# A graph network's message passing: four moves in the kernel's first iterations

## The chip, the core and the metric

The kernel runs on one core of a Trainium2 chip. The time is that of one execution on the device, in microseconds (us). The core's engines work side by side, each through its own list of instructions in order: TensorE (PE in the profile; its weight loads are PEld), VectorE (DVE), ScalarE (ACT), GpSimd (POOL), and SyncE (SP), which here only issues transfers. An engine waits where an instruction needs a result that another engine or a transfer has not delivered yet, or a buffer that another engine has not read yet.

## The reference

128 graphs of 64 nodes with 128 features each. For every pair of nodes (i, j) a message is computed by a small network of three layers with a ReLU and a layer normalisation after each of the first two; messages are kept where the adjacency matrix has a one, and summed over j. A second network of the same form takes the node and its sum, and its result is added to the node.

```python
def _mlp(x, w0, b0, g0, be0, w1, b1, g1, be1, w2, b2):
    h = jax.nn.relu(x @ w0 + b0)
    h = _layernorm(h, g0, be0)
    h = jax.nn.relu(h @ w1 + b1)
    h = _layernorm(h, g1, be1)
    return h @ w2 + b2
...
        f_i = jnp.broadcast_to(part_feats[:, :, None, :], (B, P, P, C))
        f_j = jnp.broadcast_to(part_feats[:, None, :, :], (B, P, P, C))
        pair_feats = jnp.concatenate([f_i, f_j], axis=-1)
        messages = _mlp(pair_feats, msg_w0, msg_b0, msg_ln0_g, msg_ln0_b, msg_w1, msg_b1, msg_ln1_g, msg_ln1_b, msg_w2, msg_b2)
        messages = messages * coupling_matrix[..., None]
        agg = jnp.sum(messages, axis=2)
        upd_in = jnp.concatenate([part_feats, agg], axis=-1)
        updated = part_feats + _mlp(upd_in, upd_w0, upd_b0, upd_ln0_g, upd_ln0_b, upd_w1, upd_b1, upd_ln1_g, upd_ln1_b, upd_w2, upd_b2)
```

About one pair in eight has an edge, so the kernel computes messages for the edges alone.

## The kernel before

**Units of work.** Each graph gets 640 places for edges: five tiles of 128. Two graphs are a pair (index p, 64 of them), two pairs a quad (index q, 32), four pairs a block (index b, 16). The edges are worked through in chunks of four tiles: five chunks to a quad, 160 in all. An iteration n of the main loop (line 1039) works on several chunks at once, each in another stage.

**The stages of a chunk.** `layer0(n)` (line 529) multiplies the chunk's one-hot selection matrix S by the block's rows, in two parts each (a high and a low part, `abh` and `abl`), into the PSUM bank `hps`; the ReLU on ACT (L538) empties it. `stats0` (line 540) transposes the result on PE into the bank `hT` (L544), from which DVE takes the statistics of every edge (L548). Eight iterations after layer0 comes `layer1` (line 595): a product with the bias table and the roots (L602), or four seeds by ACT (L593) instead, then four tile products (L605), and a ReLU (L608). `stats1`, `weights` and `reduce` end the messages; the class `Unit` computes the update of a block.

**What a quad needs ahead of layer1.** `var0_of(q)` (line 554) makes the variances of its 20 tiles from the statistics of its five chunks, by `square_sum` (five small POOL instructions, L245 to L249). `root_of(q)` takes the root on ACT (L255), splits it into a high part (ACT, L562) and a low part (POOL, L563); `turn_root` transposes it on PE (L568), `root_out` copies it (L573). The bias table `b1t`, made once, comes from `bias_table` (line 638: one ACT cast, L643, and four POOL instructions, L645 to L649) and five calls of `bias_part` (line 653, one POOL instruction each, L655).

**What makes S.** For a pair, `distance` (ACT, L478) and `make_tp` (DVE, L484) make the selection of its nodes; `node_rows` casts it (on ACT for the first pairs, L491, on POOL later), and `stack` sends it into S by two transfers. `marks` (PE, L509) and `compare` (DVE, L517) make the other half.

**Rows.** `rows(b, half)` (line 443) multiplies a block's nodes by the two halves of the first layer's weights into one PSUM bank (L449, L451); `rows_hi` (ACT, L463) and `rows_lo` (DVE, L469) read it. The banks at issue are `mu` (handed out by `ubank`), which `rows` uses and in which the derived weights of the early iterations are made, and `ma` (`abank`), used by `count`, `turn_x`, `turn_root` and others. Each has one buffer, so a new user waits until the last one's readers are done.

**Derived weights.** `derivation` (line 170) lists 13 small matrices made on the chip, such as `w2c` and `u2c` (L180) and `bu1b` (L203, L204). Each has an ACT step one iteration ahead, a PE product, and a copy out of PSUM one iteration later.

**The order of the work** is written by hand. `at(n, place, fn, ...)` enters a call in iteration n at a named place; within a place calls run in the order in which they were entered. The loop runs the places in this order, and each engine's instructions follow it:

```python
for n in range(last + 1):
    run(n, "a")
    run(n, "m")
...
        layer1(n - L1)
    run(n, "b")
...
        layer0(n if n >= QC else n + LEAD)
...
    run(n, "k")
...
    for k in ("x", "x1", "x2", "e0", "e1", "e"):
        run(n, k)
```

Before the loop a prologue runs chunks 0 to 2. Iterations 0 and 1 run layer0 of chunks 3 and 4; iterations 2 to 4 have no layer0; iteration 5 runs chunk 5, and from there iteration n runs chunk n. Quad 0's statistics end with chunk 4's, in iteration 3; layer1 of chunk 0 is in iteration 8. Block 0's second half of rows, `rows(0, 1)`, is in iteration 3 and is first needed by chunk 5.

**Unread products.** `keep_busy(k)` (line 909) issues k products of a constant matrix with itself into the bank `ys`, which nothing reads before the first `reduce` in iteration 18. In float32 each product is two matmuls. The prologue has 25 of them (50 matmuls at L912).

Of the kernel before, what the change touches and what calls it, by code (L numbers as in the profile page):

```python
# [23 lines left out]
def tile_gnn(  # L24
# [52 lines left out]
    PB = 4  # L77
# [207 lines left out]
    def edge_path(es):  # L285
# [18 lines left out]
        def abank():  # L304

            return ps_a.tile([P, 512], F32, name="ma")

        def ubank():

            return ps_u.tile([P, 512], F32, name="mu")  # L310
# [13 lines left out]
        def at(n, place, fn, *args):  # L324
            plan.setdefault((n, place), []).append((fn, args))
# [117 lines left out]
        def rows(b, half, k0=0, k1=4):  # L443

            blk = blocks[b]
            ps = blk["ab_ps", half] if k0 else ubank()
            for k in range(k0, k1):
                s = slice((4 * half + k) * N, (4 * half + k + 1) * N)
                nc.tensor.matmul(ps[0:N, k * C:(k + 1) * C], lhsT=blk["xnT"][:, s], rhs=w0a,  # L449
                                 start=True, stop=True)  # L450
                nc.tensor.matmul(ps[N:P, k * C:(k + 1) * C], lhsT=blk["xnT"][:, s], rhs=w0b,  # L451
                                 start=True, stop=True)
            blk["ab_ps", half] = ps
# [354 lines left out]
        for b in range(NB):  # L808
            o = b * CPB
            if b > 1:  # L810
                at(max(o - 25, 0), "a", load_adj, b)
                at(max(o - 12, 0), "a", load_x, b)
            if b > 0:
                r = max(o - 12, 1)
                at(max(o - 14, 0), "m", rank, b)
                at(r, "x", count, b)
                at(r + 1, "a", count_out, b)
                at(r + 1, "a", degrees, b)
                at(max(o - 9, r + 1), "e", place, b)
                at(*((r + 2, "a") if b == 1 else (o - 7, "e")), place_out, b)  # L820
                at(max(o - 7, 13), "m", odd_weights, b)
                at(o - 3, "x", turn_x, b)
                at(o - 2, "a", turn_x_out, b)
            for half, n in ((0, o - 2), (1, o + 3)):
                if n >= 0:
                    at(n, "x2", rows, b, half)
                    at(n + 1, "a", rows_hi, b, half)
                    at(n + 1, "m", rows_lo, b, half)
        for b in reversed(range(NB)):
            o = b * CPB  # L830
            n = o + QC + SC
# [35 lines left out]
        for p in range(NP):  # L867
            n = p * TG * 2 // CH
            if p > 1:
                if p > 2:  # L870
                    at(max(n - 7, p - 2), "a", distance, p)
                    at(max(n - 6, p - 2), "m", make_tp, p)
                at(n - 5, "a", node_rows, p)
                at(n - 4, "a", stack, p, 0, IR)
                for k in range(2):
                    at(n - 5 + k, "k", marks, p, k)
                    at(n - 5 + k, "k", compare, p, k)
                at(n - 3, "a", stack, p, 1, JR)
            w = p // 2 * QC + QC + L1 + p % 2
            last = p // 2 == NQ - 1  # L880
            at(w - 4, "a", node_marks, p)
            q, h = divmod(p, 2)
            for g in range(2):
                wait = h + 2 if q == NQ - 3 else h + 1 if q == NQ - 2 else 2 + (2 * h + g + 1) // 2
                at(*((NCHK + L1, "b") if last else (q * QC + QC + L1 + wait, "e1")), weights, p, g)
            at(NCHK + L1 + 1 if last else q * QC + SC - (q >= NQ - 3), "x1", reduce, p)
        for q in range(NQ):
            n = q * QC + QC if q else LEAD
            last = q == NQ - 1
            end = q * QC + QC + L1  # L890
            at(n, "e0", var0_of, q)
            at(*((n, "e1") if last else (n + 1, "b")), root_of, q)
            at(*((n + 2, "b") if last else (n + 1 if q else QC + 1, "x")), turn_root, q)
            at(n + 2 if q else QC + 2, "x" if last else "a", root_out, q)
            at(end - last, "e1", var1_step, q)
            wait = 0 if last else 1 if q == NQ - 2 else 2
            at(end + wait, "a", root1_of, q)
            at(end + wait, "m", inverse_of, q)
# [31 lines left out]
        place_rest()  # L930
        bias_rows()
        rows(0, 0, 0, 2)
        keep_busy(4)
        rows_hi(0, 0, 0, 2)
# [19 lines left out]

        marks_here(0)
        rows(0, 0, 2, 4)
        keep_busy(2)
        rows_here(0, 0)
# [32 lines left out]
        for n, k, bank in ([(n, k, ubank) for k, n in enumerate((1, 2, 4, 5, 6, 7, 9, 10))] +  # L991
# [6 lines left out]
            at(n - 1, "x", ahead)  # L998
            at(n, "x", keep)
            at(n + 1, "m", lambda k=k, empty=empty: empty(W.pop(("ps", k))))  # L1000
        at(3, "b", bias_table)
        for c in range(QC):
            at(4 + c, "e", bias_part, c)

# [54 lines left out]
    with ExitStack() as es:  # L1059
        es.enter_context(tc.manual_schedule())  # L1060
        flag = edge_path(es)
# [160 lines left out]
```

## Time and profile before

| | |
|---|---|
| median of 6 runs | 573.92 us (573.44 to 575.85) |
| the profiled execution | 573.96 us |
| its span, first to last instruction | 572.2 us |
| PE busy | 550.4 us, 96% |
| DVE, ACT, POOL busy | 84%, 83%, 59% |
| PE busy from 14.3 to 28.6 us | 10.54 of 14.30 us |
| mean granted TensorE clock | 0.995 |

A busy share is an average over the span; what a place in the program is worth is read from the stretch in which it lies and from what the engine there waited for. In the profile's rows, L538 is line 538 of the kernel, a tile's buffer number is left out, x4 says that a row merges four instructions, and a bracket gives the time the engine idled before the row and whose work ended that wait. A matmul's time is from its start to its last result; the next can start before that, so the spacing of starts says more of what it costs than its length.

### The profile page before, as it was taken

To read this page: it belongs to the slowest core of one execution; us is meant where nothing else is said; L and a number is where in the kernel's file an instruction comes from. 1 tells how busy PE (TensorE), PEld (TensorE's weight loads), DVE (VectorE), ACT (ScalarE), POOL (GpSimd) and SP (SyncE) were. 2 spreads that over 40 slices of the span, in tenths; PEclk is the share of its full clock that TensorE was granted. 3 is DMA by queue.
4 is the path that set the end of the run, shared out by engine and by line. 5 is a ranking of instruction groups with operands and counts; after the bars stand their busy time and mean duration, and the time that the engine had idled before them with its cause. 6 is when DMAs were issued, how large, how long until landed. Compare 5 with 4: busy or idle time off the path is not lost. (4 is left out here: it accounts for less than half of the span.)

```text
span 572.2 us, 15824 instructions
## 1 busy us (share of the span) xinstructions
PE 550.4 (96%) x5339; PEld 517.6 (90%) x5339; DVE 479.7 (84%) x1944; ACT 476.6 (83%) x1149; POOL 340.2 (59%) x898
## 2 busy tenths in 40 slices
PE   8799899999999999999999999999999999989894
PEld 8597889999999999999999999999999999979883
DVE  6768788997979899897989899797989979786686
ACT  6778879898988889898988899898888989875434
POOL 3535466765657676565657666565767656545452
PEclk9999999999999999999999999999999999998999
DMA  4475647354655745655555545447553546442101
GB/s 101 112 148 125 128 109 133 84 132 114 118 136 123 133 100 143 110 119 110 125 148 107 139 97 132 101 115 153 119 137 82 131 113 106 113 93 29 38 19 42
DMA packets 90770, 63.23 MB, mean 110 GB/s; under 512 B 57398, under 2 KB 74812, under 8 KB 90684
## 3 DMA queue, kind: packets, MB, share of 16 engines
q1 hardware_dynamic: 90396, 62.03, 48.9%
q8 instruction: 44, 0.72, 0.5%
q14 instruction: 42, 0.34, 0.2%
q10 hardware_dynamic: 288, 0.13, 0.1%
HBM read 6.82 MB, written 4.19 MB: 19 GB/s over the span
## 5 line engine op out<-in xcount | busy, mean ns | idle before, releaser
L605 PE MATMUL z<-w1c,h 128*128 128x128 f32 x1280 | 172.4, 278 | 0.0
L548 DVE BATCH_NORM_STATS2 st<-hT 128x6 f32<-128x128 f32 x640 | 141.9, 284 | 35.8 <-PE hT L544 34.3
L605 PEld LDWEIGHTS z<-w1c,h 128*128 128x128 f32 x1280 | 161.4, 192 | 8.0 <-issue 5.1
L593 ACT ACTIVATE z<-b1b,m_sd 128x128 f32<-128x128 f32 x360 | 133.7, 371 | 8.8
L615 DVE BATCH_NORM_STATS2 st<-y 128x6 f32<-128x128 f32 x640 | 137.5, 276 | 2.7 <-ACT y L608 1.4
L608 ACT ACTIVATE y<-z 128x512 f32<-128x512 f32 x160 | 94.7, 592 | 26.2 <-PE z L605 24.6
L538 ACT ACTIVATE h<-hps,b0c 128x512 f32<-128x512 f32 x160 | 109.6, 685 | 1.9 <-PE hps L535 1.9
L544 PE MATMUL hT<-ident,h 128*128 128x128 f32 x640 | 97.4, 275 | 1.8 <-DVE st L548 1.6
L678 POOL TENSOR_TENSOR w<-oh,m_q 128x320 f32<-128x320 f16 x126 | 92.0, 743 | 9.9 <-PE hT L544 5.3
L535 PE MATMUL hps<-s,abl 128*128 128x512 f32 (+3 forms) x256 | 91.6, 370 | 2.4 <-ACT h L538 2.0
L544 PEld LDWEIGHTS hT<-ident,h 128*128 128x128 f32 x640 | 76.1, 141 | 12.6 <-DVE st L548 1.9
L493 POOL CAST i<-tp 128x640 fp32r<-128x640 f16 x58 | 41.7, 719 | 67.9 <-DVE tp L484 49.0
L535 PE MATMUL hps<-s,abh 128*128 128x512 f32 (+3 forms) x256 | 78.4, 325 | 0.0
L691 PE MATMUL ys<-y,w 128*64 128x128 f32 x1280 | 76.9, 275 | 0.0
L691 PEld LDWEIGHTS ys<-y,w 128*64 128x64 f32 x1280 | 69.2, 137 | 4.2 <-issue 3.6
L245 POOL TENSOR_TENSOR m_d<-st 128x20 f32<-128x20 f32 x62 | 16.4, 264 | 88.1 <-DVE st L548 76.7
L517 DVE TENSOR_TENSOR j<-mk,cmpt 128x320 fp32r<-128x320 f32 x124 | 58.6, 472 | 1.2 <-PE mk L509 1.2
L478 ACT ACTIVATE d<-slot,mid 128x640 f16<-128x640 f16 x64 | 52.7, 824 | 0.0
L535 PEld LDWEIGHTS hps<-s,abl 128*128 128x128 f32 x256 | 49.1, 192 | 3.6 <-ACT h L538 2.7
L535 PEld LDWEIGHTS hps<-s,abh 128*128 128x128 f32 x256 | 49.2, 192 | 0.0
L469 DVE TENSOR_TENSOR abl<-mu,abh 128x512 fp32r<-128x512 f32 (+1 forms) x33 | 22.3, 675 | 31.3 <-ACT abh L463 31.1
L463 ACT CAST abh<-mu 128x512 fp32r<-128x512 f32 (+1 forms) x33 | 18.9, 573 | 24.2 <-PE mu L451 24.2
(226 smaller groups left out, 1008.9 us busy)
## 6 DMA issues: line engine op xcount, KB each, us to landing
s<-i SPq DMA_DIRECT2D x124, 160.0 KB, 2.6
s<-j SPq DMA_DIRECT2D x124, 160.0 KB, 2.6
xn<-in_x_dram SPq DMA_DIRECT2D x15, 256.0 KB, 3.6
out_dram<-uo SPq DMA_DIRECT2D x15, 256.0 KB, 2.4
an<-in_adj_dram SPq DMA_DIRECT2D x16, 128.0 KB, 2.6
oh<-tp SPq DMA_TRANSPOSE x64, 3.2
xn<-in_x_dram SPq DMA_DIRECT2D x2, 128.0 KB
out_dram<-uo SPq DMA_DIRECT2D x2, 128.0 KB, 2.6
```

Source lines behind the costliest of these rows:

```text
L478: nc.scalar.activation(D[p], slot, AF.Abs, bias=blocks[b]["mid"][:, q:q + 1], scale=-1.0)
L517: nc.vector.tensor_tensor(JR[p][:, c], MK.pop((p, k))[:, 0:HC], cmpt[:, c], op=ALU.is_equal)
L535: nc.tensor.matmul(ps[:, c:c + w], lhsT=ab[:, g % 4, :], rhs=s, start=(k == 0), stop=(k == 1))
L538: nc.scalar.activation(H[n], ps, AF.Relu, bias=b0c)
L544: nc.tensor.transpose(ps[:, t, :], H[n][:, t * P:(t + 1) * P], ident)
L548: nc.vector.bn_stats(ST0[q][:, CH * c + t, :], ps[:, t, :])
L593: nc.scalar.activation(Z[n][:, t, :], W["b1b"], AF.Copy, scale=SR[q][:, k:k + 1])
L605: nc.tensor.matmul(ps[:, t, :], lhsT=h[:, t * P:(t + 1) * P], rhs=W["w1c"], start=False, stop=True, skip_group_check=True)
L608: nc.scalar.activation(Y[n], ps, AF.Relu)
L615: nc.vector.bn_stats(ST1[q][:, CH * c + t, :], Y[n][:, t, :])
L678: (nc.vector if p == NP - 2 else nc.gpsimd).tensor_tensor(WT[p][:, :, g, :], OH[p][:, :, g * N:(g + 1) * N], Q[q][:, k:k + TG].unsqueeze(2 ...
L691: nc.tensor.matmul(YS[b][g * N:(g + 1) * N, k, :], lhsT=w[:, t, g, :], rhs=y, start=(t == 0), stop=(t == TG - 1))
```

## The change

Four edits, all of which act in the first iterations:

1. `rows(0, 1)`, in iteration 3, takes the bank `ma` instead of `mu`.
2. In iteration 5 `distance(5)` and `node_rows(4)`, both on ACT, move from place "a" to place "x", which is behind `layer0(5)`.
3. In iteration 3 `var0_of(0)` moves from place "e0" to "x", and `bias_table` from "b" to "e"; on POOL the variance of quad 0 is now ahead of the bias table. The table's ACT cast moves behind the ACT steps of the derived weights in the same iteration.
4. `keep_busy` is called at the end of iterations 2, 3, 4 and 5 with 2, 3, 2 and 2 products.

```diff
@@ rows @@
-            ps = blk["ab_ps", half] if k0 else ubank()
+            ps = blk["ab_ps", half] if k0 else abank() if (b, half) == (0, 1) else ubank()
@@ the plan of pairs @@
-                    at(max(n - 7, p - 2), "a", distance, p)
+                    at(max(n - 7, p - 2), "x" if p == PB + 1 else "a", distance, p)
                     at(max(n - 6, p - 2), "m", make_tp, p)
-                at(n - 5, "a", node_rows, p)
+                at(n - 5, "x" if p == PB else "a", node_rows, p)
                 at(n - 4, "a", stack, p, 0, IR)
@@ the plan of quads @@
-            at(n, "e0", var0_of, q)
+            at(3 if q == 0 else n, "x" if q == 0 else "e0", var0_of, q)
@@ behind the plan of derived weights @@
-        at(3, "b", bias_table)
+        at(3, "e", bias_table)
+        for n, k in ((2, 2), (3, 3), (4, 2), (5, 2)):
+            at(n, "e", keep_busy, k)
         for c in range(QC):
             at(4 + c, "e", bias_part, c)
```

## The prediction

> **What bounds the kernel now.** I read the stages first, then the waits of the head, then the head's timeline engine by engine. Stages (us, then busy time and count of PE, PEld, DVE, ACT, POOL; granted clock; DMA):
>
> ```profile
> 85.00:157.00 72.00, 72.00 (x708) 68.61 (x708) 63.88 (x262) 65.44 (x161) 46.98 (x122) 1.00 0.55 116
> 373.00:445.00 72.00, 72.00 (x738) 68.55 (x737) 63.89 (x261) 64.24 (x155) 47.43 (x127) 1.00 0.55 123
> 22.80:24.30 1.50, 0.13 (x4) 0.00 (x0) 0.77 (x3) 0.59 (x1) 1.42 (x5) 1.00 0.60 150
> 26.60:28.40 1.80, 0.21 (x3) 0.05 (x1) 1.80 (x3) 1.80 (x6) 1.80 (x2) 1.00 0.23 53
> 515.00:518.00 3.00, 3.00 (x16) 2.87 (x15) 0.28 (x1) 1.88 (x5) 0.32 (x2) 0.58 0.00 0
> ```
>
> From 85 to past 445 us PE never idles, so a microsecond that PE gains in the head arrives at the end whole, unless the tail loses it. In the head PE stands almost still twice, and the waits say for whom (total, times, longest):
>
> ```profile
> PE hps L535 <- ACT h L538: 1.6, 1, 1.6
> PE mu L180 <- DVE abl L469: 1.4, 1, 1.4
> PE ma L568 <- POOL sh L563: 0.8, 1, 0.8
> ```
>
> The timeline gives the places (start, us, instruction, idle time before it): PE, then ACT, POOL, DVE.
>
> ```profile
> 20.58 0.38 PE L208 MATMUL z<-ub0r,ones_row 1*128 1x128 f32 x2
> 20.89 0.66 PE L544 MATMUL hT<-ident,h 128*128 128x128 f32 x4
> 24.34 0.49 PE L180 MATMUL mu<-wg,mean_m 128*128 128x128 f32 x2 [1.41 <-DVE abl L469]
> 25.39 0.51 PE L535 MATMUL hps<-s,abl 128*128 128x512 f32 x1
> 26.27 0.49 PE L180 MATMUL z<-wg,mean_m 128*128 128x128 f32 x2
> 28.36 0.33 PE L535 MATMUL hps<-s,abl 128*128 128x128 f32 x1 [1.59 <-ACT h L538]
> 25.35 0.31 ACT L255 ACTIVATE m_sd<-m,eps_c 128x20 f32<-128x20 f32 x1 [1.79 <-POOL m L249]
> 26.13 0.71 ACT L491 CAST i<-tp 128x640 fp32r<-128x640 f16 x1
> 26.74 0.82 ACT L478 ACTIVATE d<-slot,mid 128x640 f16<-128x640 f16 x1
> 27.62 0.68 ACT L538 ACTIVATE h<-hps,b0c 128x512 f32<-128x512 f32 x1
> 23.88 0.25 POOL L245 TENSOR_TENSOR m_d<-st 128x20 f32<-128x20 f32 x1
> 27.73 1.09 DVE L484 TENSOR_SCALAR tp<-d,deg 128x640 f16<-128x640 f16 x1
> ```
>
> Wait one: w2c's product (L180, 24.34) takes the bank mu that the second half of the rows still holds until L469 has read it. Wait two: chunk 6 (L535, 28.36) needs bank hps, which chunk 5's relu (ACT, 27.62) empties late. ACT had hung 1.79 us on the variance (POOL, 25.35), then did a cast and a distance first. Counted from issue to issue PE could have gone on at 22.77 and at 26.59, so the waits are worth 1.57 + 1.77 = 3.34 us.
>
> **The parts.** The bank: rows(0,1) moves from mu to ma. Ma's earlier user, count(1), was copied out at 18.7; its next, turn_root(0), comes after 28 us and the rows are read by 24.7, so nothing new waits. Wait one goes. What is late next is chunk 5 itself: it needs abl, in the new order at 24.71 (below).
>
> The unread products: 2+3+2+2 = 9 of them, two matmuls each. Runs of eight such (10.03 to the next start at 10.91, 11.76 to 12.70) take 0.11 to 0.118 us each, so 18 x 0.114 = 2.05 us: 0.46, 0.68, 0.46, 0.46 in iterations 2 to 5. They wait for nothing. Were there no waits to cover them, all 2.05 us would be lost.
>
> The variance: five POOL instructions (23.88 to 25.32, 1.44 us) pass the table's four (21.60 to 23.88, 2.28 us). The table's one ACT copy (L643, spacing 0.2 us) goes behind two ACT loads of iteration 3, into idle ACT time ahead of rows_hi. Behind the table, POOL still has the root's low part (L563), then five table slices.
>
> The casts: node_rows(4) and distance(5) pass from before chunk 5's relu to behind it; they issue no DMA. The two DMAs of i(4), on SP's queue, go out 0.6 us later; chunk 10 needs them at 39.64, and they took 2.6 us to land. No other queue is crossed.
>
> **The new head, step by step**, each spacing from the rows of before. PE: the first two products stand at 20.86, so chunk 4's transposes start at 21.32 instead of 20.89. That is 0.43 lost at once: this place had no wait to fill. Rows end at 23.35 (22.92 + 0.43), the high part on ACT at 24.00, abl on DVE at 24.71. PE meanwhile: three products 23.20 to 23.88, w2c and bu1b (1.05) to 24.93, two products to 25.38, chunk 5 at 25.38 with abl ready. So chunk 5 starts as before: what the bank saves, the products fill.
>
> POOL: chunk 4's statistics end at 22.91, variance 22.99 to 24.45 (before 25.32). ACT: root 24.48, its casts and loads to 25.5, then idle until chunk 5's sums end (26.13); relu 26.16 to 26.85 (before 27.62). PE: marks, two derivation products and two unread ones from 25.97 to 27.03; chunk 6 starts there, with hps free at 26.9. Check: 28.36 - 3.34 + 2.05 = 27.07.
>
> So PE leads by 1.33 at chunk 6. What is late next: cast 26.75, distance 27.35 to 28.17 (before 27.56), so make_tp(5) waits on DVE until 28.22, and behind it in DVE's order stand u2c and chunk 5's statistics, which free the bank hT for chunk 6's transposes. make_tp takes 0.36 us alone, and 1.09 in the row of before, where POOL's table slices run (1.03 to 1.42 us each). I take 0.95, nearer to the 1.09 since the slices now run 26.89 to 32.4: end 29.15, u2c 29.35, statistics to 30.2, transposes of chunk 6 at 30.25 instead of 31.26. With 0.36 PE is the limit (30.15), with 1.09 it is 30.45: lead 0.8 to 1.1 us, value 1.0.
>
> The Trainium skill, "SBUF — State Buffer", section "SBUF: two separate sides", says the port pair that VectorE and GpSimd share is an exclusive lock for a whole instruction, and it speaks against moving distance(5) among the slices. The 1.09 us row agrees; by the rule the whole of a slice is waited for, and the sum would be 0.8 instead of 1.0.
>
> Beyond: the first layer1 would start at 32.99 - 1.0 = 32.0. Its table slices are done before: the first by 28.4, the fourth by 31.5. relu(7) at 30.5 and cu2b's copy keep ahead. The root's low part ends at 26.9, turn_root(0) comes at 28.3: cover 1.4 us. From there every row is PE-fed as before, so 1.0 us stays.
>
> **The sum.** The profiled execution took 573.96 us, span 572.2 and 1.76 around it; the median 573.92 is 0.04 under it, so its sum can stand for the median. 573.92 - 1.0 = 572.9. With the bounds of make_tp (0.8, 1.1) and of a product (0.102 us by the eight of layer1 at 520.45 to 521.27, 0.124 by the eight unread ones from 7.06 to 8.05: 18 x 0.011 = 0.2 either way), 572.5 to 573.3.
>
> **Rivals.** *Forecast, 0.50*: the head packed, 572.9.
>
> *A low-clock stretch avoided, 0.22*: after a PE wait of 1.91 us (512.3 to 514.2) the row 515 to 518 shows clock 0.58. The eight layer1 products there took 1.14 us against 0.82 at 520.45, and the work up to 519.0 together 1.6 us more than the same work later. The waits of the head, 1.41 and 1.59, drew no such drop (1.00 throughout). What decides is not in the trace; if it hangs on where the wait falls in time, a shift by 1 us may undo it, and 0.4 to 1.6 us come on top, the later waits of the tail (0.62, 1.07) taking the rest: 571.3 to 572.5. Against it: that wait itself is unchanged.
>
> The skill, "TensorE: Matmul & The Clock Gate", section "HAM oscillation — how this bites in real kernels", warns of idle gaps above about 3.4 us. By that rule alone 1.91 us should have cost nothing; the row shows it did, so I go by the row. By the rule this rival adds nothing and 572.9 stays.
>
> *Swallowed, 0.15*: make_tp(5) is held for one more table slice (1.04 us). Statistics then end at 31.2, and chunk 6's transposes start at 31.3, as before: 573.9 to 574.0. For it: POOL has slices without a gap. Against: the row of before shows one slice's wait, no second.
>
> *Slower, 0.13*: the unread products lie on PE's path and the waits come back behind them: chunk 6 starts at 28.36 + 2.05 because the relu of chunk 5 has another late source than the order on ACT (the variance, or abl). Price 2.05: 575.97. It turns to a loss once less than 2.05 of the 3.34 us of waits goes, and shows as slower above 1.15. For it: chunk 5's start gains nothing in my own layout, and the first products already push chunk 4 by 0.43. Against: in the layout abl is ready 0.67 us and ACT 0.63 us before they are needed. That the change does nothing is shut out by the two waits' releasers, which it moves.
>
> **How the numbers follow.** About 0.2%, 1.15 us, is what can be told from no change: under 572.77 is faster, over 575.07 slower. Of the forecast's 0.50, 0.18 lies under 572.77 and 0.32 above; with 0.22 faster is 0.40, with swallowed 0.15 same is 0.47, slower 0.13. The range leaves out the far end of the clock rival and most of the slower one: 571.5 to 574.8.
>
> **What would show it.** Right: w2c's product without idle time, 68 matmuls at L912 (50 before), the variance done near 24.4, chunk 5's relu at 26.2, chunk 6 at 27.0, its transposes near 30.2 held by statistics, first layer1 at 32.0. Wrong: chunk 6 at 28 or later (slower rival); transposes at 31 (swallowed); a lead of 1.0 at layer1 but another total (the tail's clock).

## The result

Beside 49 executions of the kernel before (median 574.72 us, 572.46 to 577.21) the changed kernel's 22 have a median of 572.85 us (571.75 to 575.22): a ratio of 0.9974, with a 95% interval of 0.9964 to 0.9983. By the ratio that is 1.5 us less, 1.0 to 2.1 by the interval; the medians lie 1.9 apart. The six executions known at the prediction had a median of 573.92; of the later ones about half lie near 575.4, and why is the main finding below. A second set of 12 executions (e10 below) gave 572.79, a ratio of 0.9965 (0.9945 to 0.9986).

The profiled execution took 571.68 us, span 570.0, against 573.96 and 572.2. Its timeline in the head (start, us, instruction, idle time before it), PE first, then ACT, DVE and POOL:

```profile
20.90 0.71 PE L912 MATMUL ys<-mean_m 128*128 128x128 f32 x4
21.45 0.60 PE L544 MATMUL hT<-ident,h 128*128 128x128 f32 x4
...
24.13 0.39 PE L180 MATMUL mu<-wg,mean_m 128*128 128x128 f32 x2
...
25.55 0.48 PE L535 MATMUL hps<-s,abl 128*128 128x512 f32 x1
...
27.04 0.33 PE L535 MATMUL hps<-s,abl 128*128 128x128 f32 x1
...
30.61 0.66 PE L544 MATMUL hT<-ident,h 128*128 128x128 f32 x4
...
32.41 0.50 PE L602 MATMUL z<-b1t,sdT 80*128 80x512 f32 x1
...
26.30 0.69 ACT L538 ACTIVATE h<-hps,b0c 128x512 f32<-128x512 f32 x1 [0.44 <-PE hps L535]
28.36 1.19 DVE L484 TENSOR_SCALAR tp<-d,deg 128x640 f16<-128x640 f16 x1 [0.82 <-ACT d L478]
24.18 0.23 POOL L249 TENSOR_TENSOR m<-m_d,m_s 128x20 f32<-128x20 f32 x1
```

Both waits are gone: w2c's product and chunk 6 carry no idle time any more. Chunk 6 starts at 27.04 instead of 28.36. But the lead of 1.32 us is down to 0.65 at chunk 6's transposes (30.61 against 31.26) and to 0.58 at the first layer1 (32.41 against 32.99). From there it stays: PE is full from 85 to 445 us as before, and the transposes behind the tail's wait come at 513.58 instead of 514.20. The span, though, is 2.2 us shorter, so 1.6 us more were won behind that point. The stages of the tail (busy times, then the granted clock, third from the end):

```profile
512.00:514.00 2.00, 0.42 (x4) 0.43 (x5) 0.93 (x5) 1.46 (x4) 1.59 (x6) 1.00 0.00 0
514.00:516.00 2.00, 2.00 (x19) 1.89 (x17) 0.28 (x1) 1.08 (x3) 0.20 (x1) 1.00 0.00 0
516.00:518.00 2.00, 2.00 (x21) 2.00 (x20) 1.41 (x8) 1.90 (x7) 1.37 (x3) 1.00 0.00 0
```

The wait of 1.91 us is still there, but the clock behind it is 1.00, where the kernel before had 0.58. So one execution shows two gains: 0.6 us of order and 1.6 us of clock.

### The profile page after: what moved, and what is told of

Read it like the earlier page. It is cut to its first block, busy times and chain, and to the rows that moved or that the text cites. A ratio compares the mean times of both kernels' runs of the same rounds, so it can differ in the third digit from the quotient of the medians.

```text
span 570.0 us, 15862 instructions
## 1 busy us (share of the span) xinstructions
PE 550.9 (97%) x5357; PEld 518.0 (91%) x5357; DVE 479.3 (84%) x1944; ACT 476.2 (84%) x1149; POOL 339.4 (60%) x898
```

## The experiments

Theory A: the order on the engines made the gain and the unread products are a price. Theory B: the products earn their place by keeping the clock up. Each run is read twice: by its times, and by the stretch in its profile from the start of chunk 2's transposes (17.59 us in the kernel before) to the first layer1, which leaves out the jitter of the start (16.9 to 17.8). The last column counts executions with a mean granted clock of 0.992 or less, the low mean clock of the text. Smaller differences of the mean say little: it also counts a drop behind PE's last product, which costs nothing and whose length differs (in e1's profile the clock is 1.00 up to 563 us and 0.50 over the last 5.6 us of the span, which alone makes a mean of 0.995).

| kernel | median us (executions) | ratio to before, 95% | stretch us | clock 0.992 or less |
|---|---|---|---|---|
| before, three later sets | 574.60, 574.94, 575.09 (70) | | 15.40 | 40 of 70 |
| changed, first set and e10 | 572.85, 572.79 (22, 12) | 0.9974, 0.9965 | 14.81 | 0 of 36 |
| changed, no products (e1) | 570.49 (6) | 0.9936 (0.9919 to 0.9953) | 13.46 | 0 of 6 |
| before and products (e2) | 572.33 (10) | 0.9962 (0.9949 to 0.9976) | 15.25 | 0 of 10 |
| changed, tail products (e3) | 571.25 (5) | 0.9943 (0.9928 to 0.9957) | 14.80 | 0 of 5 |
| before, tail products (e4) | 573.41 (11) | 0.9973 (0.9958 to 0.9987) | 19.26 | 5 of 11 |
| e1 with the old bank (e5) | 571.91 (8) | 0.9956 (0.9939 to 0.9973) | 14.36 | 3 of 8 |
| e1 with the old variance (e6) | 573.77 (10) | 0.9980 (0.9965 to 0.9996) | 17.96 | 5 of 10 |
| e1 with the old casts (e7) | 574.86 (10) | 1.0017 (0.9997 to 1.0036) | 14.38 | 8 of 10 |
| e1 with tail products (e8) | 570.05 (6) | 0.9931 (0.9910 to 0.9951) | 13.48 | 0 of 6 |
| e8, later turns (e9) | 569.94 (6) | 0.9912 (0.9882 to 0.9942) | 13.46 | 0 of 6 |
| changed, old variance (e11) | 571.98 (10) | 0.9951 (0.9931 to 0.9972) | 14.50 | 0 of 10 |

**e1, the changed kernel without the products.**

```diff
-        for n, k in ((2, 2), (3, 3), (4, 2), (5, 2)):
-            at(n, "e", keep_busy, k)
```

> The changed kernel without the nine unread products. Theory A (order alone made the gain, the products are paid for on PE): by the spacings of the head chunk 5 starts near 24.3 instead of 25.55, the first layer1 near 31.5 instead of 32.4, so the time is 0.9 us under the changed kernel (median near 572.0, ratio to the kernel before 0.9955 to 0.997). Theory B (the products earn by keeping the clock up): the first layer1 is early all the same, but more executions carry an added low-clock stretch of some 1.6 to 2 us (among the runs so far 5 of 22 of the changed kernel lie near 575), so that the median is at or above the changed kernel's 572.85.

Its head on PE:

```profile
24.53 0.50 PE L535 MATMUL hps<-s,abl 128*128 128x512 f32 x1 [0.35 <-DVE abl L469]
26.19 0.33 PE L535 MATMUL hps<-s,abl 128*128 128x128 f32 x1 [0.25 <-ACT h L538]
27.88 0.49 PE L208 MATMUL mu<-u0b,w2cT 128*128 128x128 f32 x2 [0.17 <-ACT w2cT L193]
31.25 0.50 PE L602 MATMUL z<-b1t,sdT 80*128 80x512 f32 x1
```

Without products the waits left are 0.35, 0.25 and 0.17 us, and the first layer1 comes 1.94 us earlier than in the kernel before by the stretch, 1.35 earlier than in the changed one. No execution has the low mean clock. The gain is larger than expected: 0.9936 instead of 0.9955 to 0.997. Of the 1.35 us about 0.3 goes with make_tp(5), which takes 0.69 us here and no longer holds chunk 6's transposes (e11 prices that). By the ratios the time gains 1.7 to 2.2 us; what that is beyond the stretch no run takes apart. Theory A holds for the changed order: there the products only cost, and none of the 18 executions without them in e1, e8 and e9 has the low mean clock.

**e2, the kernel before with the products alone**: the two lines taken out in e1, added to the kernel before.

> The kernel before with the nine unread products alone, no other edit. By the head's spacings they lie inside the two waits: chunk 6 still starts at 28.4 behind the late relu and the first layer1 at 33.0, as before. Theory A: no difference (median 573.9 to 574.7 beside the kernel before, ratio 0.999 to 1.001). Theory B: executions of the kernel before split into a group near 573.9 and one near 575.4 because the two waits of the head draw a low-clock stretch in some of them; the products fill the waits, the upper group shrinks from about half to a quarter or less, and the mean falls by 0.5 us or more.

```profile
24.25 0.49 PE L180 MATMUL mu<-wg,mean_m 128*128 128x128 f32 x2 [0.55 <-DVE abl L469]
27.62 0.33 PE L535 MATMUL hps<-s,abl 128*128 128x128 f32 x1 [0.21 <-ACT h L538]
32.26 0.51 PE L602 MATMUL z<-b1t,sdT 80*128 80x512 f32 x1
```

As laid out, the products sit inside the waits and win next to nothing on the path: a stretch of 15.25 against 15.40. Yet the time falls by 0.38% (0.24 to 0.51), and the low mean clock is gone from all ten executions. Theory B holds for the old order. So both are right, each for one kernel: the products guard a head that has waits. Not all of the fall comes from there. Five of the ten executions lie at 571.3 to 571.6 us, where only 2 of the 70 of the kernel before lie under 573.4, and the other five at 573.0 to 573.4; the profile fell on one of these and has the tail's low clock. And beside the changed kernel's 0.9974 and 0.9965 the 0.9962 is level: on top of the products the three moves of order show in the stretch (14.81 against 15.25), not in the time.

**e3 and e4, eight products in the tail's wait**, in the changed kernel and in the kernel before:

```diff
+        def keep_busy_late(k):
+            ps = ps_k.tile([P, 512], F32, name="mk")
+            for _ in range(k):
+                nc.tensor.matmul(ps[:, 0:P], lhsT=mean_m, rhs=mean_m, start=True, stop=True)
...
+                if b == NB - 4:
+                    at(n + t[10], "x", keep_busy_late, 8)
                 at(n + t[10], "x", turn, u, "uy")
```

> The changed kernel with eight unread products (about 1.8 us) in the tail's PE wait of 1.91 us ahead of the third-last full block's last transposes. If the wait is what draws the low clock of 515 to 519 us: no execution has it any more, the group near 572.8 moves to the one near 571.9, the best time stays at 571.6 to 571.8, the median is about 0.9 under the changed kernel's. If the low clock has another cause: no difference, or up to 0.2 us slower from the products.

> The kernel before with the same eight unread products in the tail's wait. If the tail's low clock was avoided in the profiled execution of the changed kernel only because its wait came 0.6 us earlier, this kernel loses it as well: span 571.0 to 571.3 when the head is clean (572.2 minus 1.0 to 1.6), median 0.9 to 1.2 us under the kernel before. The upper group (head) remains. If the drop depends on something else, no difference from the kernel before.

In e3 all five executions lie between 570.89 and 571.55, below the 571.6 to 571.8 expected for the best; the changed kernel's group at 572.4 to 573.4 (18 of 36 executions, over both its sets and the profiled ones) is missing. In e4 the lowest group moves from 573.5 to 572.0 and its tail runs at clock 1.00: the wait is what draws the low clock there, and its price is about 1.5 us. The profile of e4 fell on an execution that shows something else. Its stages in the head:

```profile
24.00:25.50 1.50, 1.50 (x9) 0.99 (x10) 0.57 (x3) 0.62 (x3) 0.65 (x4) 1.00 0.97 229
25.50:26.50 1.00, 0.88 (x5) 0.44 (x4) 0.68 (x2) 1.00 (x3) 1.00 (x2) 0.76 0.06 14
26.50:27.86 1.36, 0.00 (x1) 0.01 (x1) 1.36 (x2) 1.36 (x4) 1.36 (x2) 0.50 0.27 62
27.86:36.00 8.14, 8.14 (x32) 7.13 (x33) 3.22 (x12) 3.81 (x11) 3.35 (x4) 0.50 0.53 139
36.00:37.00 1.00, 1.00 (x6) 0.78 (x6) 0.00 (x0) 0.83 (x2) 0.00 (x0) 0.87 1.08 169
```

and PE's timeline beside it:

```profile
23.85 0.49 PE L180 MATMUL mu<-wg,mean_m 128*128 128x128 f32 x2 [1.41 <-DVE abl L469]
...
27.86 0.48 PE L535 MATMUL hps<-s,abl 128*128 128x128 f32 x1 [1.48 <-ACT h L538]
...
33.15 1.05 PE L544 MATMUL hT<-ident,h 128*128 128x128 f32 x4
...
36.36 0.51 PE L602 MATMUL z<-b1t,sdT 80*128 80x512 f32 x1
```

These are the two waits of the kernel before, 1.41 and 1.48 us. Here the clock is 0.50 from 26.0 to 36.3 us. It falls at 26.01, 0.4 us before the second wait begins (26.38), so what lay before was enough, and it stays down though PE is busy without a break from 27.86 on. Four transposes take 0.85 us from start to next start (33.15 to 34.00) instead of 0.44, and the first layer1 is 3.9 us late by the stretch. I take this to be what sets the kernel before's upper group apart: over its three later sets the 40 executions with the low mean clock average 575.4 us, the other 30 average 573.7. No profile of that kernel fell on one of them; for it speak that e4 has its head unchanged, and that e2, which acts on the head alone, has none.

Why one execution drops and another doesn't is partly in the traces. In each profile the changes of the clock lie on one grid of 3.41 us (last section), and its place against the program differs. These are the windows of the grid that hold most of the head's first wait, in the kernel before (no drop) and in e4 (drop at its end); the second number is PE's busy time:

```profile
20.57:23.98 3.41, 2.36 (x27) 1.86 (x25) 2.31 (x9) 1.76 (x6) 3.08 (x7) 1.00 0.77 192
22.60:26.01 3.41, 2.16 (x12) 1.51 (x12) 1.66 (x5) 1.59 (x5) 2.47 (x9) 1.00 0.65 153
```

Of the same 1.41 us of wait, 1.05 lie in the window in the one and 1.25 in the other.

**e5, e6 and e7, one edit undone each**, all without products:

```diff
# e5
-            ps = blk["ab_ps", half] if k0 else abank() if (b, half) == (0, 1) else ubank()
+            ps = blk["ab_ps", half] if k0 else ubank()
# e6
-            at(3 if q == 0 else n, "x" if q == 0 else "e0", var0_of, q)
+            at(n, "e0", var0_of, q)
-        at(3, "e", bias_table)
+        at(3, "b", bias_table)
# e7
-                    at(max(n - 7, p - 2), "x" if p == PB + 1 else "a", distance, p)
+                    at(max(n - 7, p - 2), "a", distance, p)
-                at(n - 5, "x" if p == PB else "a", node_rows, p)
+                at(n - 5, "a", node_rows, p)
```

> The changed kernel without the products and with the second half of the rows in bank mu again. Measured from the start of chunk 2's transposes to the first layer1, which takes the start's jitter out: 15.40 us in the kernel before, 14.81 in the changed one, 13.46 without products. If the bank is worth what its wait says: w2c's product waits for abl again (1.4 us), chunk 5 starts about 1.0 later, and the stretch is 14.2 to 14.5. If the bank is covered by the later waits for abl and the relu: 13.5 to 13.7.

> The changed kernel without the products and with the bias table ahead of the variance again. The variance then ends 1.4 to 1.9 us later and ACT hangs on it ahead of bu1b's copy and chunk 5's relu. If that edit is worth its wait: chunk 5's relu 1.0 later, the stretch from chunk 2's transposes to the first layer1 14.3 to 14.7 instead of 13.46. If ACT has room for it: 13.5 to 13.8.

> The changed kernel without the products and with distance(5) and node_rows(4) ahead of chunk 5's relu again. Two ACT instructions, 0.61 and 0.73 us by their spacing, stand ahead of the relu: chunk 6 starts 1.3 later, make_tp(5) 0.7 earlier on DVE. If the relu is the limit: stretch 14.5 to 14.9 instead of 13.46. If make_tp(5) and chunk 5's statistics are the limit: 13.0 to 13.8.

The bank is worth 0.90 us of the stretch (14.36 against 13.46), as expected. The casts are worth 0.92, less than the 1.0 to 1.4 expected, since make_tp(5) then runs in 0.42 us and chunk 5's statistics wait for PE alone. In e7 the wait ahead of chunk 6 is back at 1.59 us, and 8 of 10 executions have the low mean clock. It is slower than e1 by 4.4 us in the median (on another chip); the stretch gives 0.92 of that, and I put the rest down to the clock. For e6 the stretch can't be read, because its profile caught the low clock:

```profile
25.57 0.80 PE L180 MATMUL z<-wg,mean_m 128*128 128x128 f32 x2 [0.91 <-ACT wg L177]
```

This wait of 0.91 us had another of 0.36 a microsecond ahead of it, and the clock was 0.50 from about 25.4 to 39.0 us. What the edit is worth in the kernel with products e11 tells; without them it stays open.

**e11, the changed kernel with its products and the old variance**, the edit of e6:

> The changed kernel, products kept, with the bias table ahead of the variance again. Without products this order drew a low clock in the head in the execution that was profiled, 25 to 38 us. If the products guard against that: head at clock 1.00, and no execution at or below 0.992. The stretch from chunk 2's transposes to the first layer1, 14.81 in the changed kernel, tells the edit's own worth: 15.2 to 15.6 if the variance holds chunk 5's relu, 14.8 to 15.0 if the products hide it.

The stretch is 14.50, neither of the two expected: 0.31 shorter than the changed kernel's. make_tp(5) on DVE says why; the row of the changed kernel is above (1.19 us):

```profile
27.95 0.39 DVE L484 TENSOR_SCALAR tp<-d,deg 128x640 f16<-128x640 f16 x1 [0.71 <-ACT d L478]
```

With the table first, POOL's slices start at 25.66 instead of 26.87 us, 8.46 after chunk 2's transposes instead of 9.27, and make_tp(5), at the same distance from chunk 2's transposes in both (10.75 and 10.76 us), comes 0.13 us before the end of a slice (28.08), where in the changed kernel it comes 0.02 behind the start of one (28.34) that runs to 29.37. The variance's own lateness is covered by the products: ACT waits 1.13 us for it and still reaches chunk 5's relu when the sums are there. So in the kernel with products this edit costs 0.3 us of the stretch (the times, 571.98 against e10's 572.79, go the same way, but their intervals overlap); no execution of e11 has the low mean clock, so there the products guard it.

**e8 and e9, towards a better kernel.** e8 is e1 with the tail's products of e3. In e9 the roots of quads 1 and 2 are also turned behind layer1 instead of ahead of it:

```diff
-            at(*((n + 2, "b") if last else (n + 1 if q else QC + 1, "x")), turn_root, q)
-            at(n + 2 if q else QC + 2, "x" if last else "a", root_out, q)
+            at(*((n + 2, "b") if last or q in (1, 2) else (n + 1 if q else QC + 1, "x")), turn_root, q)
+            at(n + 2 if q else QC + 2, "x" if last else "k" if q in (1, 2) else "a", root_out, q)
```

> The changed kernel without the nine products of the head and with eight in the tail's wait. If the head needs no products once its waits are gone, and the tail's low clock is drawn by its wait: stretch 13.46 as without products, no low clock from 510 to 520 us, times in one group near 569.8 to 570.3, median 0.3 to 0.7 us under that of the kernel without products (570.49). If the head's products are needed against the low clock, an upper group 1.5 us or more above.

> The kernel of the tail's products alone, and the roots of quads 1 and 2 turned one product group later (turn_root behind layer1 instead of ahead of it). PE waits 0.83 and 1.47 us for POOL there. If every PE wait ahead of the full stretch counts whole, about 1.6 us come on top (0.83 and 0.8 of the 1.47): median near 568.4 to 568.7, ratio to the kernel before 0.989 to 0.991. If the waits only move (the roots' copy is late for layer1 or the bank ma for the next transposes): 569.8 to 570.3 as without it.

e8 has no low clock in the tail, and four of its six executions lie between 569.76 and 570.12; two lie at 571.9 and 572.1 with the same mean clock. Its median is 0.44 us under e1's, on another chip, so e8's ratio of 0.9931 against 0.9936 doesn't tell the two apart. In e9 the waits only move (start, us, instruction, idle time before):

```profile
44.48 0.50 PE L602 MATMUL z<-b1t,sdT 80*128 80x512 f32 x1 [0.35 <-ACT sdT L573]
...
56.11 0.31 PE L568 MATMUL ma<-ident,sh 128*80 128x128 f32 x1 [0.57 <-POOL sh L563]
58.95 0.66 PE L435 MATMUL ma<-ident,xn 128*128 128x128 f32 x4 [1.39 <-ACT sdT L573]
```

The 0.83 and 1.47 us for POOL become 0.35, 0.57 and 1.39, the last because block 2's transposes need the bank that the later copy still holds. e8 and e9 are level (570.05 and 569.94), and both beat the kernel before. Against the changed kernel beside it on the same chip (e10) the interval of e9 is barely clear (it ends at 0.9942, e10's begins at 0.9945); that of e8 (to 0.9951) is clear of the first set (from 0.9964) and not of e10.

**e10, the changed kernel again**, beside e9 and e11 on one chip:

> The changed kernel itself, beside the others on one chip. Order and clock together: median 572.3 to 573.1, 2 us or more above the kernel with the tail's products alone and without the head's; no execution with the mean clock at or below 0.992 that the kernel before shows in half of its own; a group near 571.9 and one near 572.9, with and without the tail's low clock. If the earlier gap of 2.4 us to the kernel without the products came from another chip: within 1 us of it.

572.79 us, its stretch 14.79 and make_tp(5) again 1.19 us, and no low mean clock in 12 executions: the gap of 2.85 us to e9, beside it on that chip, is not the chip's.

## Why the prediction came out as it did

**The number** was 572.9 and the median is 572.85, inside 571.5 to 574.8. The forecast gain of 1.0 us was too small, however: set against all executions of the kernel before it is 1.5. That it fits is in part luck: the six executions it started from held only one near 575.4, where later sets have more than half with the low mean clock (40 of 70). By the prediction's own line (572.77) the median is just not faster; by the ratio the gain is 0.26%, and its interval (0.17 to 0.36) is clear of no change but reaches below the 0.2% that was to be told. I had put more on no difference than on faster.

**Head gains reach the end**: right. 0.58 us at the first layer1 are 0.62 at the tail's wait.

**Bank and casts**: right in kind. The two waits vanish together, and undone one by one they are worth 0.90 and 0.92 us.

**The products' price**: put at 2.05 us, measured 2.25 from start to next start (0.55, 0.77, 0.47, 0.46). The layout held: chunk 5 at 25.55 (25.38 laid out), chunk 6 at 27.04 (27.03).

**make_tp(5)**: the wait was seen, its size was not. I took 0.95 us between 0.36 and 1.09; it was 1.19, because it started 0.14 later (28.36), just behind the start of a slice, and waited that slice out. Statistics of chunk 5 end at 30.55 instead of 30.2, and the lead shrinks to 0.58 where 0.8 was the low end. The Trainium skill's page "SBUF — State Buffer" (section "SBUF: two separate sides"), which the prediction cited, has the shared ports locked for a whole instruction. The 1.19 us here against 0.39 in e11 agree.

**The clock is the step that failed.** The prediction put it so: "The waits of the head, 1.41 and 1.59, drew no such drop (1.00 throughout)." That was true of the one execution profiled. But 40 of 70 executions of the kernel before have the low mean clock, and e4's profile shows the same waits draw it. Hence the larger part of the gain: with the waits of the head filled or removed, none of the changed kernel's 36 executions shows the low mean clock, and 40 of 70 times the 1.7 us between the groups is an estimated 1.0 us in the mean. I had the clock as a rival (0.22), but only for the tail, and that part came true as well: the profiled execution lost the tail's drop. The prediction said "What decides is not in the trace", but a good part of it is. These are the windows of the clock's grid that hold most of the tail's wait, in the kernel before and in the changed one:

```profile
512.09:515.50 3.41, 1.50 (x13) 1.24 (x12) 1.74 (x9) 2.54 (x7) 1.80 (x6) 1.00 0.00 0
511.97:515.38 3.41, 1.80 (x16) 1.74 (x16) 1.24 (x6) 2.07 (x5) 1.78 (x6) 1.00 0.00 0
```

Before, the whole wait lies in one window, and the clock falls at its end; in the changed kernel the wait comes 0.62 us earlier, the window only 0.12, and 0.30 us of the wait fall into the window ahead. The other profiles with this wait bear it out: whole in one window it drew the drop in e2 and e7, cut by an edge it drew none in e5, e6, e10 and e11; only e1, with 1.90 of 1.91 us in one window, has none. So in the profiled execution the shift did undo it, but not in most: of the 36 executions only 11 lie at or under 572.05 us, and the 18 of the group that e3 removes would, by their times, still have it.

**Swallowed and slower**: neither came, though make_tp(5) did wait out a slice, which is what the first feared. The first products do push chunk 4's transposes by 0.55 us (21.45 against 20.89), as feared, but the waits that went were larger.

**Open**: seven of the changed kernel's 36 executions lie at 574.9 to 575.4 us with a mean clock of 0.994, and two of e8's 2 us above its others. No profile fell on one of them.

## What to carry to other kernels

A wait on PE ahead of a long stretch that PE fills is worth its whole length, plus what the clock does after it; so look at the mean clock of every execution, not only at the one profiled. Remove such waits by order first: unread products then cost time (1.35 us of the stretch here), while they pay where a wait has to stay (2.2 us in the old order, part of it from the tail's clock, and about 1.5 in the tail). An instruction moved on one engine must be costed where its consumer then lands: make_tp(5) cost 0.39 or 1.19 us by which side of a POOL instruction it fell on.

## What the runs showed of the hardware

- A wait of 1.41 us, with one of 1.48 after 2.5 us of work, went with a halved TensorE clock for 10.2 us (26.01 to 36.25, e4), and waits of 0.36 and 0.91 us went with one of 13.7 us (25.36 to 39.01, e6), most of it with PE busy without a break. The tail's wait of 1.91 us did it for 3.4 us (515.50 to 518.91 in the kernel before).
- These lengths are three, four and one times 3.41 us, and in every profile with several changes of the clock all of them lie on one grid of that step: in the kernel before 515.50, 518.91 and 570.11 us (15 steps later), in e4 26.01, 36.25 and 568.73 (156 steps later). The Trainium skill's page "TensorE: Matmul & The Clock Gate" (section "What's actually happening") gives a window of 3413 ns for the clock's monitor, which fits. It has the clock fall after at least one idle window and rise after at least one busy one. Here it fell after windows in which PE idled for a part: 1.25 of 3.41 us in e4, 1.06 in e6 (21.94 to 25.36), 1.91 in the tail. It rose in e4 only behind the second window that PE filled (29.43 to 36.25), in e6 behind the third (28.77 to 39.01), in the tail behind the first.
- No single idle share fits all places: 1.05 us in a window of the head drew no drop (20.57 to 23.98 in the kernel before), and neither did 1.46 in the changed kernel at 54.58 to 57.99. What else counts is not shown.
- The same program with the same waits has the low mean clock in some executions and not in others: 5 of 11 in e4, 8 of 10 in e7.
- A DVE instruction of 0.36 to 0.39 us took 1.19 where a POOL instruction of 1.0 us and more ran (28.36 us in the changed kernel), and 0.39 in the same place of the order a little earlier against POOL's (e11).
